# A longer gather time in the clock that places list products

## The chip, the cores and the metric

The kernel runs on one core of one Trainium2 chip. The metric is the device time of one execution in microseconds. Three timed runs of the kernel before gave a median of 2307.89 us (2305.75 to 2312.35); a profiled execution of it, the only source of times of single instructions, took 2333.96 us.

## The reference

Four graph layers over N = 2708 nodes with D = 512 features share one sparse 0/1 adjacency `adj`, each followed by a residual sum and a layernorm. The change concerns layer 2, which applies this twice (`W_stack` has two entries):

```python
proj = x @ W
Wh, Ws = jnp.split(proj, 2, axis=-1)
scores = Wh @ Ws.T
a = jax.nn.softmax(scores, axis=-1) * adj
out = a @ Wh
out = out + x
return jax.nn.leaky_relu(out, NEG_SLOPE)
```

Layers 0, 1 and 3 are products of `adj` with the features, then with a weight; layer 3 follows the second attention layer directly.

## The kernel before

**Tiles.** Nodes are 22 blocks of 128 rows. Columns of the score matrix come in six chunks (`CH`, line 28): four of 512, one of 384, one of 276. A chunk has four, three or three blocks of nodes (the last block has 20 rows).

**One attention layer** (`Attention.layer`, line 1801) goes over the chunks k = 0 to 5, and for each over 22 slots, one block j of scores a slot: `scores` (line 1534) is eight records of matmul on TensorE into a PSUM bank, copied out by ScalarE. In the slots of chunk k the chunk before it is finished: `soften` (line 1605) subtracts the column maximum, takes the exponential, adds to the sum, multiplies by the mask and stores the tile with SyncE's queue into a DRAM tensor `pairs[k % 2]`, where the value rows Wh already lie. Two such tensors are in use, so chunk k may be stored only when everything of chunk k - 2 has been gathered.

**List products.** The adjacency is sparse, so `a @ Wh` isn't done densely. For each block of 128 nodes a list of neighbours was made earlier (`givers`). `fetch` (line 1659) issues one indirect DMA from GpSimd's queue, which gathers 128 rows (Wh beside the softened weights) into one of 11 buffers (`WIDES`, line 43). `weigh` (line 1706) issues one list product on TensorE: either a *single* (one gather, two matmul records) or a *group* of four quarters (four gathers, eight records that run side by side in the array). A full block has four singles and then two groups: six products, 12 gathers. In this document c.b is block b of chunk c, "s" a single and "g" a group. At most ten gathers are issued ahead of the products (`AHEAD`, line 1373). After a block's last product `end` (line 1742) adds the residual on VectorE, which also needs a row tile `xr` that SyncE's queue loads when the block's first gather is issued (line 1665).

**What sets the order.** Every engine executes in the order in which the Python code issues (`Ordered`, line 54). Where a product is issued is decided while the program is built, by a clock: `advance` adds an estimate to `self.clock` for each piece of TensorE work (`cost`, line 488: 3.41 us for the scores of a 512-column slot; 0.85 for a single, 1.1 for a group). `fetch` writes down when it believes a gather done: it starts when the gather before it has passed, takes 1.15 us of the queue, and lands 6 us later (lines 1683 to 1685). `weigh` returns without a product if the believed landing lies in the future, unless it is called with `True`, which *forces* the product. After each slot up to three products are tried. What is left over after the last slot goes into the layer's tail: there `until` (line 1870) alternates softening of the last chunk, list products that are due, and *fill*. In the first attention layer the fill is the projection work of the second (`second`, line 1876). In the second it is the beginning of layer 3 (`early`, line 604): units of eight matmuls (`multiply`, four node blocks, each in a high and a low part `xh`, `xl`), called L3 units here. `prepare` makes `xh` on ScalarE and `xl` on VectorE. Before certain units `need` (line 1864) forces products until the normalised rows that layer 3 takes as input have been issued: rows of chunk 3 ("need 15"), later rows of chunk 4 ("need 18").

Within the slots, the products of the chunk three back are finished by force at slot n = 3 (in `layer`), before the first `soften` of the chunk after it, so what `soften` asserts (line 1613) holds there at any rate. The last chunk of a layer is softened in the tail, without that step: there it is the clock alone that has to have placed all gathers of chunk 3 by then.

Of the kernel before, what the change touches and what calls it, by code (L numbers as in the profile page):

```python
# [49 lines left out]
def rows_of(i):  # L50
    return min(P, N - i * P)
# [1315 lines left out]
class Attention:  # L1367
# [237 lines left out]
    def soften(self, ch):  # L1605


        nc, v, cw = self.nc, ch.softened, ch.cw
        ch.softened += 1
        if v < NB:  # L1610
            if v == 0 and ch.k >= 2:

                assert not self.chunks[ch.k - 2].to_fetch
            n = rows_of(v)
            s = ch.s[v][:n, :cw]
            nc.vector.tensor_sub(s, s, ch.shift[:n, :cw])
            nc.scalar.activation(s, s, AF.Exp)
        j = v - 1
        if j < 0:
            return  # L1620
        n = rows_of(j)
        s = ch.s[j][:n, :cw]
        if j == 0:
            ch.sum = self.page(f"sum{ch.name}")
            nc.vector.tensor_copy(ch.sum[:, :cw], s)
        else:
            nc.vector.tensor_add(ch.sum[:n, :cw], ch.sum[:n, :cw], s)
        nc.vector.tensor_mul(s, s, ch.masks.pop(j)[:n, :cw])
        to = ch.ly.pairs[ch.k % 2][j * P : j * P + n, :]
        if cw == BANK:  # L1630
            nc.sync.dma_start(
                to[:, : 2 * PAIR].rearrange("j (r x) -> j r x", x=PAIR)[:, :, D:],
                ch.s[j][:n, :].rearrange("j (r x) -> j r x", x=2 * P),
            )
            return
        for r in range(2):
            w = min(2 * P, cw - r * 2 * P)
            nc.sync.dma_start(
                to[:, r * PAIR + D : r * PAIR + D + w],
                ch.s[j][:n, r * 2 * P : r * 2 * P + w],  # L1640
            )
# [17 lines left out]
    def fetch(self, ch):  # L1659


        q, t = ch.to_fetch.pop(0)
        g = self.f.wide(f"g{ch.name}_{q}_{t}")
        i, _, w = ch.blocks[q]
        if q not in ch.x:
            ch.x[q] = self.page(f"xr{ch.name}_{q}")
            given = self.k.saved[1] if ch.ly.number == 0 else self.k.between
            self.nc.sync.dma_start(ch.x[q][:w], given[i][:w])
            if ch.ly.number == 1:
                ch.first[q] = self.page(f"x1{ch.name}_{q}")  # L1670
                self.nc.sync.dma_start(ch.first[q][:w], self.k.saved[1][i][:w])

        h = t // ONLY if t < QUARTERS * ONLY else (QUARTERS - 1, 0)[q % 2]
        first, width = (D + P + h * QW, D + P - h * QW) if q % 2 else (0, D + (h + 1) * QW)
        self.nc.gpsimd.indirect_dma_start(
            out=g[:, :width],
            out_offset=None,
            in_=ch.ly.pairs[ch.k % 2][:, :],
            in_offset=bass.IndirectOffsetOnAxis(ap=self.k.givers[:, i, t : t + 1], axis=0),
            element_offset=(q // 2) * PAIR + first,  # L1680
        )

        begin = max(self.fetch_free, self.clock + (16 if (q, t) == ch.first_fetch else 0))
        self.fetch_free = begin + 1.15
        ch.fetched.append((g, self.fetch_free + 6))

    def fetch_ahead(self):
# [272 lines left out]
```

## Time and profile before

| | us |
|---|---|
| median of three timed runs | 2307.89 |
| profiled execution | 2333.96 |
| its span, first to last instruction | 2332.2 |
| TensorE busy | 2281.0 (98%) |
| VectorE busy | 1408.7 (60%) |
| GpSimd busy | 705.9 (30%) |
| of it 510 gathers | 525.0 |
| ScalarE busy | 675.3 (29%) |
| mean granted TensorE clock | 0.994 |

By stages of the span: layers 0 and 1 and the first projections to 768 us; first attention layer's slots to 1269, its tail to 1472; second attention layer's slots from 1472 to 1964, its tail to 2124; the rest of layer 3 to 2332. A busy TensorE is counted with modelled ends of matmuls, so a stretched group of products still counts as busy.

### The profile page before, as it was taken

The numbers are of one execution on the slowest core, as the hardware profiler recorded it, in microseconds if no ns is written. First come the engines' busy times: TensorE is split into PE (matmuls) and PEld (weight loads), VectorE is DVE, ScalarE is ACT, GpSimd is POOL, SyncE is SP. The second block draws the span as 40 slices with busy tenths as digits, with TensorE's granted clock in tenths as the row PEclk, the third lists the DMA queues.
The fourth block names the chain that finished last, engine by engine and source line by source line (L and its number), as shares of the span: only waits on it lengthen the run. The fifth ranks groups of instructions, "written<-read, shape, count | busy, mean of one in ns | idle before, by whom it ended". The sixth has DMA issues, their size and how long they took to land.

```text
span 2332.2 us, 25904 instructions
## 1 busy us (share of the span) xinstructions
PE 2281.0 (98%) x8525; PEld 1291.3 (55%) x8525; DVE 1408.7 (60%) x2803; ACT 675.3 (29%) x1354; POOL 705.9 (30%) x822
## 2 busy tenths in 40 slices
PE   9999999999999999999999999999999998899997
PEld 6676777777645444343555444444343454466685
DVE  6777886787554446857666511247868777534523
ACT  7444352222111123222222200123233233342221
POOL 3333431111000002534556540001634556442000
PEclk9999999999999999999999999999999999999999
DMA  9966752223557314867879997314867889873311
GB/s 349 283 186 185 186 169 79 75 79 103 205 200 267 119 45 167 309 203 276 282 268 375 326 411 301 143 41 175 291 208 270 295 284 360 270 225 117 121 50 43
DMA packets 260929, 486.34 MB, mean 209 GB/s; under 512 B 40238, under 2 KB 126950, under 8 KB 260784
## 3 DMA queue, kind: packets, MB, share of 16 engines
q1 hardware_dynamic: 192128, 269.63, 33.2%
q0 software_dynamic: 68656, 214.96, 28.2%
q8 instruction: 69, 1.13, 0.2%
q14 instruction: 76, 0.62, 0.1%
HBM read 307.55 MB, written 176.92 MB: 208 GB/s over the span
## 4 chain that ended last, share of the span: by engine, by line
PE 83%; DVE 6%; DMA 4%; issue 3%; POOL 1%; ACT 1%; another core or an unknown queue 1%; SPq 0%; POOLq 0%; DVEq 0%; ACTq 0%
PE sp L71 30%; PE acc L71 29%; PE mm L71 8%; PE z L71 6%; PE wst L71 6%; DMA g<-pairs,givers 1%; POOL g L71 1%; DVE s L71 1%; DMA at<-in_adj_t 1%; DMA x<-in_x 1%; DVE sum L71 1%; PE mix L71 1%; PE list L71 1%; PE tr_x2b L71 1%
## 5 line engine op out<-in xcount | busy, mean ns | idle before, releaser
L71 PE MATMUL sp<-xs,wst_sb 128*128 128x512 f32 (+3 forms) x2112 | 798.6, 545 | 0.4 <-issue 0.4
L71 POOL DMA_INDIRECT g<-pairs,givers x510 | 525.0, 1029 | 897.7 <-issue 399.7
L71 PEld LDWEIGHTS sp<-xs,wst_sb 128*128 128x128 f32 (+1 forms) x2112 | 379.6, 186 | 409.1 <-issue 341.8
L71 PE MATMUL acc<-m,xh 128*128 128x512 f32 (+4 forms) x1584 | 569.1, 381 | 8.4 <-ACT m L71 5.9
L71 PE MATMUL acc<-m,xl 128*128 128x512 f32 (+4 forms) x1584 | 552.1, 366 | 13.4 <-issue 10.9
L71 PEld LDWEIGHTS acc<-m,xh 128*128 128x128 f32 (+1 forms) x1584 | 289.3, 189 | 74.7 <-issue 23.6
L71 PEld LDWEIGHTS acc<-m,xl 128*128 128x128 f32 (+1 forms) x1584 | 289.6, 189 | 59.3 <-issue 17.2
L71 PE MATMUL acc<-g 128*32 128x512 f32 (+1 forms) x1020 | 268.2, 606 | 6.9 <-DMA g<-pairs,givers 3.5
L71 ACT ACTIVATE s<-s 128x512 f32<-128x512 f32 (+3 forms) x264 | 151.8, 580 | 339.6 <-DVE s L71 213.6
L71 ACT COPY s<-sp 128x512 f32<-128x512 f32 (+2 forms) x252 | 132.2, 527 | 392.8 <-PE sp L71 298.1
L71 DVE TENSOR_TENSOR top<-top,s 128x512 f32<-128x512 f32 (+2 forms) x240 | 149.4, 622 | 155.8 <-ACT s L71 123.3
L71 PE MATMUL mm<-w,ht 128*128 128x512 f32 (+1 forms) x528 | 225.0, 594 | 4.0 <-DVE ht L71 4.0
L71 ACT CAST m<-at 128x512 fp32r<-128x512 uint8 (+5 forms) x396 | 199.6, 567 | 70.0 <-DVE r L71 14.5
L71 DVE TENSOR_TENSOR s<-s,shift 128x512 f32<-128x512 f32 (+3 forms) x264 | 162.8, 620 | 38.4 <-ACT shift L71 27.3
L71 DVE TENSOR_TENSOR s<-s,a 128x512 f32<-128x512 f32 (+3 forms) x264 | 165.9, 628 | 10.0 <-issue 0.9
L71 DVE TENSOR_TENSOR sum<-sum,s 128x512 f32<-128x512 f32 (+4 forms) x252 | 156.9, 623 | 15.9 <-ACT s L71 13.6
L71 PEld LDWEIGHTS mm<-w,ht 128*128 128x128 f32 (+1 forms) x528 | 95.9, 186 | 122.6 <-issue 111.9
L71 PEld LDWEIGHTS acc<-g 128*32 128x32 f32 (+1 forms) x1020 | 75.2, 135 | 153.4 <-issue 124.5
L71 PE MATMUL z<-w,xt 128*128 128x512 f32 (+1 forms) x352 | 151.0, 596 | 0.0
L71 PE MATMUL wst<-xt,mixed 128*128 128x512 f32 (+2 forms) x384 | 150.5, 544 | 0.0
L71 POOL DMA_DIRECT2D x<-o x44 | 26.0, 597 | 353.2 <-DVE o L71 349.0
L71 DVE SCALAR_TENSOR_TENSOR xr<-acc,rden,xr 128x512 f32<-128x512 f32 (+1 forms) x44 | 32.8, 747 | 140.0 <-PE acc L71 77.5
(168 smaller groups left out, 1533.5 us busy)
## 6 DMA issues: line engine op xcount, KB each, us to landing
pairs<-z_sb SPq DMA_DIRECT2D x84, 768.0 KB
pairs<-s SPq DMA_DIRECT2D x168, 256.0 KB
at<-in_adj_t SPq DMA_DIRECT2D x84, 256.0 KB
xres<-x POOLq DMA_DIRECT2D x44, 256.0 KB
x<-o POOLq DMA_DIRECT2D x43, 256.0 KB
pairs<-s SPq DMA_DIRECT2D x84, 128.0 KB
x<-x SPq DMA_DIRECT2D x37, 256.0 KB
at<-mask SPq DMA_DIRECT2D x32, 256.0 KB
```

Source lines behind the costliest of these rows:

```text
L71: ins = call(*args, **kw)
```

## The change

Two edits. In `fetch`, the believed time of a gather on its queue goes from 1.15 to 1.3 us. In `soften`, an assertion that chunk k - 2 has been gathered completely becomes a loop that forces list products until it has been. No instruction is added or removed; what changes is where the clock places the products, and with them the gathers, the row loads and the block ends that they trigger.

```diff
         if v < NB:
             if v == 0 and ch.k >= 2:
 
-                assert not self.chunks[ch.k - 2].to_fetch
+                while self.chunks[ch.k - 2].to_fetch:
+                    self.weigh(True)
             n = rows_of(v)
...
         begin = max(self.fetch_free, self.clock + (16 if (q, t) == ch.first_fetch else 0))
-        self.fetch_free = begin + 1.15
+        self.fetch_free = begin + 1.3
         ch.fetched.append((g, self.fetch_free + 6))
```

## The prediction

> **What bounds the kernel now.** I read the page's busy times first, then TensorE by stages, then the timelines of TensorE, GpSimd and VectorE where TensorE is idle.
>
> Busy times on the page; then TensorE by stage (columns: stretch, us, busy and records, granted clock, DMA share, GB/s):
>
> ```profile
> PE 2281.0 (98%) x8525; PEld 1291.3 (55%) x8525; DVE 1408.7 (60%) x2803; ACT 675.3 (29%) x1354; POOL 705.9 (30%) x822
> ```
> ```profile
> 0.00:900.00 900.00, 889.95 (x3816) 1.00 0.52 167
> 900.00:1400.00 500.00, 493.41 (x1619) 1.00 0.85 300
> 1400.00:1640.00 240.00, 240.00 (x628) 1.00 0.46 164
> 1640.00:2125.00 485.00, 462.25 (x1614) 0.98 0.81 272
> 2125.00:2332.00 207.00, 195.37 (x853) 0.98 0.21 71
> ```
>
> TensorE bounds it. Its idle time is 51 us: 21.7 in stretches without gathers, 6.6 in the first gather stretch, 22.8 in the second. Only these 29.3 us, plus groups that are stretched while they wait, can be touched. The TensorE timeline shows where most of it is:
>
> ```profile
> 1955.10 1.68 PE L71 MATMUL acc<-g 128*32 128x512 f32 x8
> ...
> 1963.72 0.77 PE L71 MATMUL acc<-m,xh 128*128 128x512 f32 x1
> 1974.41 0.79 PE L71 MATMUL acc<-m,xl 128*128 128x512 f32 x1 [9.92 <-issue]
> ...
> 1993.81 4.07 PE L71 MATMUL acc<-g 128*32 128x512 f32 x8 [0.42 <-issue]
> 1998.19 4.76 PE L71 MATMUL acc<-g 128*32 128x512 f32 x10 [0.31 <-issue]
> ```
>
> A group normally takes 1.06; at 1955 it takes 1.68, at 1993 and 1998 over 4: these wait for gathers. The first L3 unit of the tail waits 9.92 for `xl`. VectorE tells why, GpSimd tells the pace of gathers:
>
> ```profile
> 1970.26 0.75 DVE L71 SCALAR_TENSOR_TENSOR xr<-acc,rden,xr 128x512 f32<-128x512 f32 x1 [8.60 <-issue]
> 1973.67 4.90 DVE L71 SCALAR_TENSOR_TENSOR xl<-x,xh 128x512 fp32r<-128x512 f32 x8
> ...
> 2009.88 0.75 DVE L71 SCALAR_TENSOR_TENSOR xr<-acc,rden,xr 128x512 f32<-128x512 f32 x1 [15.80 <-remote]
> ```
> ```profile
> 1984.93 0.95 POOL L71 DMA_INDIRECT g<-pairs,givers  x1 [3.62 <-PE acc L71]
> 1986.19 0.95 POOL L71 DMA_INDIRECT g<-pairs,givers  x1 [0.31 <-issue]
> 1987.45 0.95 POOL L71 DMA_INDIRECT g<-pairs,givers  x1 [0.30 <-issue]
> ```
>
> The end of block 3.2 stands ahead of `xl` on VectorE. Gathers leave every 1.256 us (0.953 + 0.30), not 1.15.
>
> **What the Trainium skill says.** (1) "Perfetto Trace Analysis", DMA Instruction — SWDGE (GPSIMD): such a DMA's record ends when descriptors are written, not when data is there. The trace agrees: the gather of 1996.58 (record 0.95) lands at 2000.0, 3.4 after its start; with DMA share 1.00 products stall up to 5.2 after the record's end. (2) "DMA: Bandwidth & Descriptors", Anatomy of one DMA — SWDGE: about 2.0 us plus bytes at 436 GB/s; for 128 rows of 2.2 to 2.6 KB that is an estimate of 2.7, against 2.5 from record end here. (3) "TensorE: Matmul & The Clock Gate", Part 1: an idle window of some 3.4 us halves the clock. It agrees: after the 9.92 idle, L3 matmuls start 0.43 apart instead of 0.229. (4) "Perfetto Trace Analysis", Tensor Engine Instruction: matmul ends are estimates. It agrees: the products of 4.0 end by the records at 2000.8, yet VectorE is released at 2009.88.
>
> **A discount.** The profiled execution is 26.1 us longer than the median. Work without gathers has no reason to differ, so I put most of the 26 into the gather stages: of their 29.3 idle plus some 10.6 of stretching, about 14 us remain in a timed run. Sums below are first against 2333.96, then against 2307.89.
>
> **The change, step by step.** The clock is plain arithmetic; I followed it product by product at both rates. At 1.15 it gives, for the slots of the third chunk, products per slot 0 0 3 1 1 2 3 1 3 2 1 3 2 1 1, just what the timeline from 928 us shows.
>
> *The loop in `soften`.* It runs only in the first layer's tail: three products (3.2g, 3.3s, 3.3s), all due by the clock. Price 0; cover: projections fill TensorE there (100% busy from 1280 to 1472). Chunk 5's first stores wait behind the last gather of chunk 3 on SyncE's queue, up to 5 us, ahead of later row loads and z stores; nothing on TensorE needs these within 10 us. Uncovered it would cost 5.
>
> *Slots.* The number of products in chunks 2 to 4 stays 24; they come up to two slots later. Stalls before or in products there sum to 9.8 us (1.35, 1.71, 1.85 in the first layer, 1.63, 0.71, 1.40, 1.13 in the second). Seven microseconds more of believed queue time over 48 gathers (48 x 0.15) cover these. Gain in the profile 9.8; in a timed run between 0 and 9.8, and since the 14 us are used up below, I take 2.
>
> *Chunk 5's slots hold 16 products, not 20.* In both layers 3.2's groups and 3.3's first two singles move into the tail. First layer: fill covers them, 0. Second layer: there the tail is bound by gathers. When the slots end, all of chunk 3's gathers have been issued before, and 16 are missing up to the fourth single of 4.1, which "need 15" forces; after, 26 are missing. Walk, t = 0 at the end of slot 21's scores (1960.7), single 0.86, group 0.99, L3 unit 1.83, gather 1.256 and 3.5 to land, a buffer free 0.3 after the product eleven gathers back. Before: the gathers of 4.0 start at 12.3 (GpSimd is still busy with 3.3), 4.0's last at 26.1, the last needed at 31.1, and that product ends at 35.5. After: 3.3's remaining gathers start only as 3.2g frees buffers, at 6.1; 4.0's first at 18.7, its last at 32.6, the last needed at 37.6, product done at 42. One group fewer (1.0) lies ahead of t = 0. **Loss 42 - 1 - 35.5 = 5.5.** The same walk gives 4 at 1.05 a gather, and 2.6 at 1.4 with 5 to land (the end of the tail then costs 7.1 instead of 4).
>
> *`xl` in front.* Block 3.2's end is issued after the first L3 units now, so `xl` no longer stands behind it. In the profile that saves 8.5 of idle and some 3 of half clock. But without the late semaphore the end costs only 3.6 of VectorE (four of 0.7 to 0.75, plus small), and TensorE, arriving 3.7 earlier, waits for its own four `xl` (0.61 apart). By the same walk the wait is 3.3 before, 3.1 after. Timed gain 0 to 11; I take 0.
>
> *More softening ahead.* The clock runs on while products are forced, so 11 instead of 9 softening steps stand ahead of the `prepare` for rows 12 to 15. Each takes 1.19 on VectorE; TensorE already waits there (3.07 at 2031.8). **Loss 2.4** (0 if cover returns).
>
> *End of the tail.* 4.1g moves from L3 unit 13 to 18, and at the end 5.1g, 5.1g and three singles are left after the last unit and forced, with 12 gathers to issue from the first 5.0g on. Walk from 5.0's last single: gathers end their issue at 21.8, product done at 25.1 against 21.2 of TensorE work. **Loss 4.0.** Layer 3's next rows come 9.2 after the last product (2123.46 to 2132.67), covered by 11 us of units: 0.
>
> **Sum.** Losses 11.9. In the profile: -9.8 - 8.5 - 3 + 11.9 = -9, some 2325. Timed: +11.9 - 2 = +9.9; gathers may go faster without the profiler, so I cut the 9.5 of the two gather walks by 2: +8, **2316**. What is late next is GpSimd's queue in the second layer's tail.
>
> **Rivals.** *A wash:* without the profiler gathers pass at about 1.05 (tail losses 4 + 2.4 + 2.2) and half the slot stalls are real (-5): +3.6, about 2311.5. For it: a clock that fits gathers better and a kernel 98% bound by TensorE. Against it: ten gathers did move behind the slots. *Faster:* the 9.92 wait and the slot stalls are real in timed runs too: -9, about 2299. Its place is VectorE's order at the start of the second tail, its price 11.5; it decides once over 10 of the 21 us in the two gains survive without the profiler. For it: the wait is the longest in the trace. Against it: the 26 us have to come from somewhere. *The change does nothing:* excluded, since four products leave chunk 5's slots.
>
> **Chances.** About 0.3% (7 us) is what a measurement of this kernel can tell from no change. Forecast 0.48, wash 0.36, faster 0.16. Upper end: 6 to land everywhere (the two walks then give 12.2), no gain: 12.2 + 2.4 = 14.6, 2322.5. Lower end: 2300, most of the faster rival. Likeliest case alone: 2315 to 2323.
>
> **What would show it.** Right: no stretched groups in the slots; `xl` not behind a block end; groups of 3.3 and 4.0 stretched in the second tail, more gathers after 1960, and stalls at 5.1g before 2125. Wrong: a timed gain with these, which means the discount failed; or groups of 4.0 that don't wait.

## The result, and the profile after

| | before | after | ratio, 95% interval |
|---|---|---|---|
| timed runs, median of four each, one chip (A below) | 2306.98 us | 2323.11 us | 1.0064 (1.0052 to 1.0077) |
| profiled execution | 2333.96 us | 2323.33 us | |

The change makes the kernel some 16 us slower: the forecast's side, twice its size, and just above the upper end of the stated range (ratio 1.0064, where 2322.5 us is 1.0063). The profiled execution of after is one of its timed runs. That of before, 26 us longer than its timed runs, is none of those; on which chip it was taken isn't known.

The page's busy times of the kernel after, then TensorE by stage as shown for before (stretch, us, busy and records, granted clock, DMA share, GB/s):

```profile
PE 2281.3 (98%) x8525; PEld 1292.7 (56%) x8525; DVE 1410.9 (61%) x2803; ACT 673.2 (29%) x1354; POOL 700.6 (30%) x822
```
```profile
0.00:900.00 900.00, 890.42 (x3815) 1.00 0.52 167
900.00:1400.00 500.00, 498.08 (x1633) 1.00 0.86 302
1400.00:1640.00 240.00, 240.00 (x634) 1.00 0.46 164
1640.00:2125.00 485.00, 468.54 (x1645) 0.99 0.80 273
2125.00:2321.00 196.00, 184.21 (x803) 0.98 0.20 67
```

TensorE does the same work. Idle is 1.9 us in the first gather stretch (6.6 in the profile of before) and 16.5 in the second (22.8). No group of products is stretched in the slots of chunks 2 to 4. What is left stands in the second layer's tail. TensorE's timeline there from 1950 to 2045, the lines with more than 0.5 us of idle time:

```profile
1952.72 0.50 PE L71 MATMUL acc<-m,xh 128*128 128x512 f32 x1 [1.51 <-ACT m L71]
1953.87 0.50 PE L71 MATMUL acc<-m,xl 128*128 128x512 f32 x1 [0.65 <-DVE xl L71]
1973.28 4.26 PE L71 MATMUL acc<-g 128*32 128x512 f32 x8 [0.80 <-DMA g<-pairs,givers]
1989.47 6.29 PE L71 MATMUL acc<-g 128*32 128x512 f32 x14 [1.63 <-DMA g<-pairs,givers]
2017.11 0.79 PE L71 MATMUL acc<-m,xh 128*128 128x512 f32 x1 [6.83 <-ACT m L71]
2028.59 0.50 PE L71 MATMUL acc<-m,xh 128*128 128x512 f32 x1 [1.00 <-ACT begun L71]
```

`xl` no longer stands behind a block end (0.65 instead of 9.92). The second group of 3.3 takes 4.26 instead of 1.06. The longest wait is now the one before the first unit of rows 12 to 15, 6.83; in the profile of before it was less than half of that:

```profile
2031.79 0.50 PE L71 MATMUL acc<-m,xh 128*128 128x512 f32 x1 [3.07 <-ACT m L71]
```

ScalarE's timeline of the kernel after tells what that unit's `xh` waited for:

```profile
2002.34 0.62 ACT L71 CAST m<-at 128x512 fp32r<-128x512 uint8 x1 [7.31 <-DMA x<-r]
2002.98 1.28 ACT L71 ACT_TABLE_LOAD   x1
...
2015.60 0.43 ACT L71 ACTIVATE s<-s 128x276 f32<-128x276 f32 x1 [0.76 <-DVE s L71]
2015.94 0.61 ACT L71 ACTIVATE xh<-x 128x512 fp32r<-128x512 f32 x1
```

Between the mask's cast and `xh` stand the 11 softening exponentials, 1.19 apart; before each of them ScalarE waits for VectorE (0.76). GpSimd's pace in the tail, then the last products, forced with gathers missing, and the last groups in the profile of before:

```profile
1987.33 0.95 POOL L71 DMA_INDIRECT g<-pairs,givers  x1 [0.30 <-issue]
1988.58 0.95 POOL L71 DMA_INDIRECT g<-pairs,givers  x1 [0.30 <-issue]
```
```profile
2108.13 2.17 PE L71 MATMUL acc<-g 128*32 128x512 f32 x4 [0.28 <-DMA g<-pairs,givers]
2111.11 2.95 PE L71 MATMUL acc<-g 128*20 128x512 f32 x6 [0.81 <-DVE xr L71]
```
```profile
2117.67 1.90 PE L71 MATMUL acc<-g 128*32 128x512 f32 x10
```

A gather still leaves every 1.26 us: in this profile, which has none of the first one's long waits in the slots, it isn't faster.

### The profile page after: what moved, and what is told of

Same layout as the page of the kernel before. It is cut to its first block, busy times and chain, and to the rows that moved or that the text cites. A ratio compares the mean times of both kernels' runs of the same rounds, so it can differ in the third digit from the quotient of the medians.

```text
span 2321.3 us, 25909 instructions
## 1 busy us (share of the span) xinstructions
PE 2281.3 (98%) x8525; PEld 1292.7 (56%) x8525; DVE 1410.9 (61%) x2803; ACT 673.2 (29%) x1354; POOL 700.6 (30%) x822
## 4 chain that ended last, share of the span: by engine, by line
PE 84%; DVE 6%; DMA 5%; issue 2%; ACT 2%; POOL 1%; SPq 0%; DVEq 0%; ACTq 0%; POOLq 0%
PE sp L71 32%; PE acc L71 29%; PE mm L71 8%; PE z L71 6%; PE wst L71 6%; DVE s L71 1%; DMA x<-in_x 1%; DMA g<-pairs,givers 1%; DMA mask<-some 1%; DMA at<-in_adj_t 1%; DVE sum L71 1%; PE mix L71 1%; PE list L71 1%; DMA pairs<-s 0%; ACT m L71 0%
## 5 line engine op out<-in xcount | busy, mean ns | idle before, releaser
L71 POOL DMA_INDIRECT g<-pairs,givers x510 | 519.4, 1018 | 897.7 <-PE acc L71 246.4
L71 PEld LDWEIGHTS wst<-xt,mixed 128*128 128x128 f32 x384 | 71.9, 190 | 72.3 <-issue 60.5
```

What stands on the lines that cost most here:

```text
L71: ins = call(*args, **kw)
```

## The experiments

They ran on three chips, B (first four), C (next four) and D (last four), each with the kernel before beside them. A stands for the chip of the first timed runs and of the profile of after; that it is none of these three is likely from the times, but isn't known. The kernel before took 2330.7 us on B, 2330.3 on C, 2325.9 on D (medians of 59 to 67 runs, from 2318 to 2346), against 2307 on A. So ratios are compared within a chip where possible, and a comparison across chips is said to be one. Two tables gather what the profiles say, worked out from the starts of TensorE's records; the single experiments follow.

**Elapsed time by stage**, from the first scores record of one chunk to that of another, the same instructions in all kernels (the last column ends at one fixed L3 matmul, some 11 us after the last product):

| profile | layer 1: chunks 2 to 4 | chunk 5 and tail | layer 2: chunks 2 to 4 | chunk 5 and tail |
|---|---|---|---|---|
| before, first profile | 284.0 | 271.6 | 281.2 | 234.4 |
| before again (B) | 281.6 | 272.3 | 280.1 | 226.8 |
| after (A) | 280.3 | 269.3 | 276.8 | 233.2 |
| after again (C) | 280.3 | 274.8 | 278.0 | 245.3 |

**Losses of the second layer's chunk 5 and tail**: elapsed less an estimate of the unstalled TensorE work up to the same place (single 0.86, group 0.99, L3 unit 1.83, scores record 0.2475, and some 3 for transposes and divisors; 196.6 in all). The estimate is off by a constant in each column, -1 to -2 in the first and some +1.8 in the last, so only differences within a column count. Columns: slots 0 to 5; from there through the forced products and the first four L3 units after them (the gather walk); the next four units and the wait before rows 12 to 15 that ends them; on to unit 40; the end.

| profile | slots 0-5 | gather walk | rows 12-15 | to unit 40 | end | sum |
|---|---|---|---|---|---|---|
| before, first profile | -2.1 | 23.1 | 9.4 | 4.9 | 2.7 | 38.0 |
| before again (B) | -1.6 | 19.1 | 5.3 | 4.9 | 2.7 | 30.4 |
| before, 11 steps (D) | -1.7 | 17.0 | 5.8 | 4.9 | 2.7 | 28.7 |
| before, 3 steps (C) | -0.8 | 19.1 | 0.0 | 5.5 | 2.7 | 26.5 |
| tail only (B) | -2.1 | 18.9 | 1.3 | 4.7 | 2.4 | 25.2 |
| chunk 5 shift, 9 steps (C) | -1.8 | 19.4 | 4.3 | 4.6 | 2.5 | 29.0 |
| after (A) | -1.8 | 20.7 | 6.9 | 4.9 | 6.2 | 36.9 |
| after again (C) | 5.4 | 22.0 | 10.0 | 4.9 | 6.7 | 49.0 |
| after, 9 steps (B) | 6.9 | 19.2 | 3.5 | 4.9 | 6.7 | 41.2 |
| after, 3 steps (C) | 6.3 | 20.9 | 1.4 | 1.2 | 6.9 | 36.7 |
| after, 9 steps, short tail (D) | 4.8 | 22.4 | 3.0 | 4.9 | 2.7 | 37.8 |
| after, chunk 4 early (D) | -0.8 | 21.3 | 5.9 | 4.2 | 5.6 | 36.2 |

**The kernel before, profiled again** (no edit).

> The kernel before, unchanged, profiled once more. Theory (the discount): the first profile of it was disturbed, so this execution ends near 2307, 3 us at most from its timed runs; TensorE's stalls in the slots of both attention layers sum to under 3 us instead of 9.8, and the wait for xl at the start of the second tail is about 3 us instead of 9.92. Rival: the waits belong to the program; the execution ends near 2334 again, with stalls of about 10 us in the slots and a wait for xl of about 10.

Measured: 2323.8, where its timed runs on that chip stand at 2330.7. TensorE's timeline, the two places of the first profile's longest waits:

```profile
1964.55 0.50 PE L71 MATMUL acc<-m,xl 128*128 128x512 f32 x1 [1.53 <-DVE mv L71]
...
2021.82 0.80 PE L71 MATMUL acc<-m,xh 128*128 128x512 f32 x1 [5.22 <-ACT m L71]
```

The wait for `xl` is 1.53, not 9.92. The stalls at products in the slots sum to some 6, not 9.8; the theory had under 3. So the first profile's longest wait was an accident of one execution, as the theory said. But its reason was wrong: on B, C and D the timed runs themselves take 2326 to 2331, and the execution whose trace is read is no longer than the others. The 20 to 26 us don't belong to that one execution; they part the runs on A from all others. Whether the chip makes them, or something else that differed there, no run tells.

**The first layer alone.**

```diff
-        self.fetch_free = begin + 1.15
+        self.fetch_free = begin + (1.3 if ch.ly.number == 0 else 1.15)
```

> 1.3 for the gathers of the first attention layer, 1.15 for those of the second. Theory: the second layer makes the whole difference; here 2305 to 2307 (ratio 0.999 to 1.000), since the loop in soften is covered by projections and the few stalls in the first layer's slots are worth 2 at most. Rival: the forced products and the row loads behind them on SyncE's queue cost in the first layer too, about 5 us (1.002). Second rival: the 4.9 us of slot stalls of the first layer were real, a gain of 5 (0.998).

The loop in `soften` is in. Measured: 2329.4 beside 2330.7, ratio 0.9993 (0.9977 to 1.0009). The first layer costs nothing that can be measured here, 2 us at most, and the loop, which runs in it alone, shows no cost either. In its profile the slots of chunks 2 to 4 are 1 us shorter than before's, and chunk 5 with its tail 2 longer.

**Two softening steps less in the kernel after.**

```diff
-        done = self.clock + (2 if ly.number == 0 else 4)
+        done = self.clock + (2 if ly.number == 0 else 6.8)
```

> The kernel after, with the pace of the last softening set back by two steps, so that 9 steps stand ahead of the prepare for rows 12 to 15 as before, not 11; the placement of every product stays that of the kernel after. Theory: the steps stand on the path that sets the end, 1.19 each: 2.4 us faster than after, 2320.7 (1.0058 of before), and TensorE's wait at that prepare falls from 6.8 to about 4.4. Rival: the wait is set by something else (the load of x, the norm): same time as after (1.0070), same wait. Second rival: the half clock after that wait goes as well: 5 us faster, 1.0045.

Measured: 2332.6 beside 2330.7, ratio 1.0007 (0.9992 to 1.0022). The wait before rows 12 to 15 is half that of the two profiles of after (6.83 above, 7.91 in the next):

```profile
2025.61 0.50 PE L71 MATMUL acc<-m,xh 128*128 128x512 f32 x1 [3.41 <-ACT m L71]
```
```profile
2034.53 0.79 PE L71 MATMUL acc<-m,xh 128*128 128x512 f32 x1 [7.91 <-ACT m L71]
```

Against the kernel after on chip C (1.0036, below) this is 0.0029 less, some 7 us, nearer to the second rival; but it is a comparison across chips. What that rival rests on isn't seen either: after the shorter wait the half clock is still there, and the way to unit 40 loses 4.9 as before.

**The tail alone.**

```diff
-        self.fetch_free = begin + 1.15
+        self.fetch_free = begin + (1.3 if self.in_tail else 1.15)
...
+        self.in_tail = ly.number == 1
```

> 1.15 everywhere except in the second attention layer's tail, where it is 1.3: slots, the forced products and the 9 softening steps stand as before; only the products from the groups of 4.1 on come later, and at the end one group of 5.1 and three singles of 5.2 are forced with gathers missing (after: two groups and three singles). Theory: this is the prediction's end of the tail, at most its 4.0: 2 to 4 us slower than before (1.001 to 1.0017). Rival: later placement is what costs most of the 16: 10 or more (1.004). Second rival: 0, gathers land in time.

Measured: 2330.2 beside 2330.7, ratio 0.9995 (0.9979 to 1.0011): the second rival. Forcing one group and three singles at the end costs nothing that shows (2.4 against 2.7 in the table; the interval ends at 2.6 us); with a second forced group, as in after, the profiles lose 3.5 to 4 more.

**The kernel after, again** (no edit).

> The kernel after, unchanged, beside the kernel before. Theory: what the change costs depends on the chip. Where TensorE's signals come late in the gather stages, as in the first profile and on the chip of the runs so far (before at 2331), the longer time also hides stalls in the slots; the kernel after with two softening steps less stood at 1.0007 there, so with them it should be 2.4 to 5 us slower than that: 1.002 to 1.003. On a chip like that of the first timed runs (before at 2307) it is 1.0064 again. Rival: the cost belongs to the program alone, and the ratio is 1.006 to 1.007 on either.

Measured: 2339.9 beside 2330.3, ratio 1.0036 (1.0022 to 1.0049). Half of A's cost, as the theory said, a little over its 1.003. The part that A's profile doesn't have lies at the start of chunk 5. TensorE in the kernel after on A, then on C, then ScalarE on C:

```profile
1895.44 2.03 PE L71 MATMUL sp<-xs,wst_sb 128*128 128x276 f32 x8
1897.30 0.49 PE L71 MATMUL tr_mx<-ident,wide 128*128 128x128 f32 x3
```
```profile
1901.26 2.03 PE L71 MATMUL sp<-xs,wst_sb 128*128 128x276 f32 x8
1907.68 0.88 PE L71 MATMUL tr_mx<-ident,wide 128*128 128x128 f32 x3 [4.39 <-DVE rs_v L71]
```
```profile
1900.65 0.39 ACT L71 COPY s<-sp 128x276 f32<-128x276 f32 x1 [4.10 <-remote]
1905.65 0.39 ACT L71 COPY s<-sp 128x276 f32<-128x276 f32 x1 [4.61 <-remote]
```

By the records the second block of scores ends at 1900.9; ScalarE is released at 1905.65, 4.8 us later. On A the same copy starts 0.2 after. VectorE waits alike for the column maxima, and TensorE for VectorE:

```profile
1906.39 0.56 DVE L71 TENSOR_REDUCE mx<-tr_top 128x3 f32<-128x384 f32 x1 [5.63 <-remote]
```

Then TensorE's granted clock is 0.67 from 1910 to 1915. Such late releases tell the profiles apart. In those from B, C and D and in the first profile of before, 15 to 24 of ScalarE's 252 copies of scores start over 1 us late, counted from the end of their scores by the records or of ScalarE's work before them, whichever is later; all of them lie in chunks 2 to 5, and there the trace has only 64 to 78% of the semaphore updates that TensorE's records name. In the profile of after on A no copy is late and no update is missing. The ends of matmuls are modelled, so the records alone don't tell whether TensorE is later than they say or only its signals are.

**Three steps, in the kernel before.**

```diff
-        done = self.clock + (2 if ly.number == 0 else 4)
+        done = self.clock + (2 if ly.number == 0 else 12.4)
```

> The kernel before, with the pace of the last softening set back by six steps: 3 instead of 9 steps stand ahead of the prepare for rows 12 to 15, all else in the tail as before but for two groups of 4.1, which come after two or three more steps. Theory: the steps are on the path as long as TensorE waits at that prepare (0.6 to 5.5 us in the profiles of before and of its variants with the same tail); six steps are 7.1 us of VectorE, so the whole wait goes and some half clock with it: 3 to 5 us faster than before (0.998). Rival: no wait in timed runs, or the later end of the softening holds up the gathers of chunk 5: 0 to 4 slower (1.000 to 1.002).

Measured: 2323.1 beside 2330.3, ratio 0.9973 (0.9954 to 0.9992), the theory. The wait before rows 12 to 15 is gone (0.0 in the table). Six steps gave 7.2 us by the medians, 1.2 a step, as much as a step takes on VectorE; the interval runs from 2 to 11. This version beats both kernels on that chip.

**Three steps, in the kernel after.** The same edit with 15.2.

> The kernel after, with the same pace set back by eight steps: 3 instead of 11 steps ahead of that prepare; products stand as in the kernel after. Theory: TensorE's wait of 6.83 there in the profile of after goes whole, and the half clock after it (some 2): 7 to 9 us faster than the kernel after beside it. Rival: only the 2.4 that the prediction gave to the steps is on the path: 2 to 3 faster.

Measured: 2331.9, ratio 0.9999 (0.9984 to 1.0014): 8.0 us by the medians faster than after on the same chip (1.0036), the theory. The wait of 7.91 is gone (the column falls from 10.0 to 1.4), and 3.7 less are lost up to unit 40. But with 3 steps in both, after is still 8.8 slower than before (2331.9 against 2323.1), nearly the 9.5 that it is with 11 and 9. So this wait costs both kernels almost alike, and explains little of the difference between them: that it makes the rest of A's 16 isn't borne out on C.

**Only the slots of chunk 5 in the second layer.**

```diff
-        self.fetch_free = begin + 1.15
+        self.fetch_free = begin + (1.3 if ch.ly.number == 1 and ch.k == 3 else 1.15)
...
-        done = self.clock + (2 if ly.number == 0 else 4)
+        done = self.clock + (2 if ly.number == 0 else 6.8)
```

> 1.3 only for the gathers of chunk 3 of the second attention layer, so that the slots of its chunk 5 hold 17 products instead of 20, with the softening set back so that 9 steps stand ahead of the prepare for rows 12 to 15 as before; the first layer and the other slots are those of before. Theory: this is the prediction's first gather walk alone, 5.5 us of waits in the groups of 3.3 and 4.0, less 3 of TensorE work already counted there: 4 to 6 us slower than before (1.002 to 1.0025), with some 10 us of stretched groups before the first product of 4.1. Rival: gathers catch up while TensorE does L3 units, 0 to 1 (1.000).

Measured: 2330.4 beside 2330.3, ratio 0.9996 (0.9975 to 1.0017), the rival. Three products moved into the tail cost nothing that shows (gather walk 19.4 against 19.1); the interval, -6 to +4 us, excludes 5.

**Eleven steps, in the kernel before.** The softening edit with 1.2.

> The kernel before, with the pace of the last softening set forward by two steps: 11 instead of 9 steps stand ahead of the prepare for rows 12 to 15; the only other shift is none, every product stays. Theory: two steps cost what they gave back when taken out of the kernel after (7 us there: 3.4 of wait and the half clock that a longer wait brings): 4 to 8 us slower than before (1.002 to 1.0035). Rival: the prediction's term, 2.4 (1.001).

Measured: 2327.8 beside 2325.9, ratio 1.0009 (0.9992 to 1.0025), 2.1 us. The rival, the prediction's own 2.4; 6 and more are excluded, but the interval holds 0 too. TensorE waits 5.70 before rows 12 to 15.

**Early lists and three steps.**

```diff
-        self.fetch_free = begin + 1.15
+        self.fetch_free = begin + (1.3 if ch.k < 2 else 1.15)
...
-        done = self.clock + (2 if ly.number == 0 else 4)
+        done = self.clock + (2 if ly.number == 0 else 12.4)
```

> 1.3 only for the gathers of chunks 0 and 1 of both attention layers, whose products lie in slots with room behind them; 1.15 for the rest, and 3 softening steps ahead of the prepare. Theory: the gains of both without the losses: the wait at the prepare (6 us, as measured with 3 steps in the kernel before) and the stalls in the slots of chunks 2 and 3 (0.7 to 3.7 us in the profiles of before): 0.996 to 0.997 of before. Rival: stalls in the slots cost nothing in timed runs: 0.9973, the same as with 3 steps alone.

Measured: 2322.3 beside 2325.9, ratio 0.9984 (0.9972 to 0.9996). It beats before too, but by no more than three steps alone did on C: that stalls in the slots are worth anything isn't shown.

**The kernel after with 9 steps and a short tail.**

```diff
-        self.fetch_free = begin + 1.3
+        self.fetch_free = begin + (1.0 if self.in_tail else 1.3)
...
+        self.in_tail = ly.number == 1
...
-        done = self.clock + (2 if ly.number == 0 else 4)
+        done = self.clock + (2 if ly.number == 0 else 6.8)
```

> The kernel after with 9 softening steps, and with the believed gather time at 1.0 in the second layer's tail alone: the products from the groups of 4.1 on come earlier and none of chunk 5 is left to be forced after the last L3 unit. Theory: the end of the tail costs its predicted 4.0 (stalls of 3.7 at 5.1's group and 5.2's singles in the profiles of after): 3 to 5 us faster than the kernel after with 9 steps (1.0007 of before), so 0.9985 to 0.9995. Rival: the gathers are late anyway and the stalls only move to other products: the same 1.0007.

Measured: 2328.2 beside 2325.9, ratio 1.0008 (0.9997 to 1.0019). In its profile the end loses 2.7 again and not 6.7, as the theory has it; in the ratio nothing of that shows against the 1.0007 of B, so the time doesn't confirm it. The two stand on different chips, and each interval is over 2 us wide to either side: inconclusive.

**The kernel after with chunk 2's lists as before.**

```diff
-        self.fetch_free = begin + 1.3
+        self.fetch_free = begin + (1.15 if ch.k == 2 else 1.3)
```

> The kernel after, with 1.15 for the gathers of chunk 2 only, so that the last groups of chunk 2 stand in slots 18 and 19 of chunk 4 and not in 20 and 21. Theory, on a chip where TensorE's signals come late: those last groups delay the signals that ScalarE and VectorE wait for at the start of chunk 5, and TensorE waits 4.5 us at the transposes of wide in the first layer and some 5 in the second; these go, and stalls of 1 to 3 in chunk 4's slots come back: 4 to 8 us faster than after beside it (1.0036 of before there), so 1.0003 to 1.002. On a chip with early signals: no such waits in the profile of after, no difference. Rival: the waits are there wherever these groups stand, no difference on either.

Measured: 2329.2 beside 2325.9, ratio 1.0016 (1.0004 to 1.0029), 4.6 us under the 1.0036 of C, as the theory had it, across chips. The profile is clearer:

```profile
1899.92 2.03 PE L71 MATMUL sp<-xs,wst_sb 128*128 128x276 f32 x8
1903.04 0.52 PE L71 MATMUL tr_mx<-ident,wide 128*128 128x128 f32 x3 [1.10 <-issue]
```

TensorE waits 1.10 at the maxima's transposes instead of 4.39; slots 0 to 5 lose -0.8 instead of 5.4 (4.8 on the same chip D in the run before this one, with the groups in slots 20 and 21), and the first layer's chunk 5 with its tail takes 268.3 instead of 274.8. So the wait at the maxima depends on where chunk 2's last groups stand. On A the same place cost nothing, so the late releases are needed too. And part of the gain is paid back earlier: the first layer's chunks 2 to 4 take 284.6 instead of 280.3.

## Why the prediction was right or wrong

**What bounds the kernel, and where the cost lies: right as far as can be told.** TensorE does the same work. On A the kernel before leaves, if its other stages took what they take in the profile of after, 217 us for the second layer's chunk 5 and tail (233.2 less the 16 of the timed runs); if its slots had stalls there, less. Then all of the 16 lies in the stage where the forecast put its losses. That is an inference and isn't shown: no profile of before was taken on A.

**The discount: right in effect, wrong in reason.** The 9.92 wait was not what other executions had; without the discount the sum would have been -9, so the discount alone gave the forecast its sign. That this held on A is luck: the reason given, the profiler, isn't borne out. Every run on B, C and D has the first profile's length within some 1%, and every profile from there has its late releases. The prediction also took one of these, VectorE's release at 2009.88 some 9 us after the products of 4.0, for a matmul's modelled end; but TensorE's later records start from 2000.7 on, and the profile of after on A has no such delay at all. The sum for the first profile's own conditions failed too: on C the kernel after takes 2338.8 of span where -9 gave some 2323. Of its gains, the stages of the slots give 3 to 9 (0.9 to 4.4 in the first layer, 2.4 to 4.4 in the second), less than the 9.8; the 11.5 at `xl` was the accident of one execution (waits of 1.2 to 4.4 in the repetitions); and a wait at the maxima's transposes that no step named takes 7 in the second layer's slots 0 to 5.

**The signs to look for: right.** No stretched groups in the slots, `xl` not behind a block end, stretched groups of 3.3 and 4.0 in the second tail, stalls at 5.1's group before 2125: the profile of after has them all. Both rivals fall with the timed runs of after, on A and on C: there is no gain, and the wash's 1.0016 lies below both intervals.

**The loop in `soften`: right within 2 us.** The first layer alone measures 0.9993.

**Slots.** The stretched groups are gone, as forecast. The gain of 2 in timed runs isn't seen; on A it can't be separated.

**Chunk 5's slots, 5.5.** Too large where it could be tried: 0 within 4 us on C for three of the four products; in the profiles the gather walk costs the six kernels of after's kind 21.1 on average, and 18.7 the six later ones that have before's lists up to there (before again, the first layer alone, the tail alone, 11 steps, 3 steps, early lists: 19.1, 19.1, 18.9, 17.0, 19.1, 19.1), so 2.4; with the first profile's 23.1 it would be 1.7. The walk itself was close: it put the fourth single of 4.1 at 42 after slot 21's scores; on A it ends at some 44.

**More softening ahead, 2.4: it fits, but isn't shown.** +2.1 us for two steps in the kernel before (interval -1.9 to +5.8), and 2.1 between the averages of that column for the kernels with 9 steps in before's tail (9.4, 5.3, 6.0 in the first layer alone, 1.3) and after's with 11 (6.9, 10.0, 5.9), which scatter by more than that. What the prediction passed over is the whole wait: against 3 steps, 9 in the kernel before and 11 in after cost 6 to 8 us on C, and setting the softening back takes it away.

**End of the tail, 4.0: right in the profiles.** 2.7 before, and 6.2 to 6.9 in the four profiles that have after's tail. With one forced group and the same singles it was 0, so the second group seems to make it. In timed runs the term isn't seen: the short tail gained nothing that shows.

**Why only half the size: the weak step is the sum's last line.** The 11.9 of losses was cut to 8 for a gain in the slots (2) and for gathers that go faster without the profiler (2). The second cut has no ground: gathers leave every 1.26 us on A as well. The first isn't seen, though on A it couldn't be told apart. Without both cuts the forecast would have been 4 nearer. The other 4 of the missing 8 are open in any case, and more than these if the walk costs on A what it costs elsewhere. On A the gather walk and the wait for rows 12 to 15 together must cost after some 12 more than before (16 less 3.5 to 4 for the end), if the inference above holds, where the prediction had 7.9 and the profiles of B to D show 4.5. Either of the two may lose less in the kernel before on A than anywhere else; a profile of it on that chip would tell, and there was none.

**On other chips** the forecast of +8 was met for a reason that it didn't have: 1.0036 on C is 8.4 us, made of the new wait at the maxima (7, and 2.5 in the first layer), the three losses (8.3) and the slots' gains (-3 to -9); these are sums from single profiles, which scatter by several us, so the list isn't a balance.

## What to carry to other kernels

Before a profile that is longer than the timed runs is trusted for its longest wait, profile the same kernel again: that wait may be one execution's. When work is held back by a planned clock, look for what already stands in the slots that it moves into (here, where releases came late, the maxima's transposes of the next chunk), and for what the held back clock lets through in a burst on another engine. A wait that both kernels share can be worth more than the one that the change is about: six softening steps moved behind a `prepare` gave 7 us on C, and 4 on D together with the early lists.

## What the runs showed of the hardware

The same program took 2307 us in the first timed runs (four, within 7 us) and 2326 to 2331 on B, C and D, where 59 to 67 single runs spread over 20 to 27 us. For the kernel after, whose profiles from A and C can be compared, the whole difference of 17.5 us in span lies in the stages with gathers: 5.5 in the first layer's chunk 5 and tail, 1.2 in the second layer's chunks 2 to 4 and 12.1 in its chunk 5 and tail, less some 1.4 outside. These are also the stages of the late releases and the missing updates. The gather queue's share is the same (28.1 to 28.5% in all profiles), so the transfers' own time doesn't explain it; what does stays open.

After idle times of 3.41 us (after with 9 steps) and 6.83 us (after on A) TensorE's granted clock was 0.50 until 7.3 and 5.7 us after work went on, and records of L3 matmuls took 0.63 instead of 0.39. The shorter wait didn't cost less of it: the way to unit 40 lost 4.9 in both.
